# Attention scores of a unit accumulated in one PSUM bank per head with key differences, and some additions of exponentials moved to VectorE

## The chip, the cores and the metric

The kernel runs on one core of a Trainium2 chip. The metric is the device time of one execution in microseconds (us). The median of three runs of the kernel before is 2413.94 us (2413.16 to 2414.01). The profile shows one profiled execution of the same program; its span is 2411.0 us.

The names of the engines in the profile: PE is TensorE (matmuls), PEld its weight loads, DVE is VectorE, ACT is ScalarE, POOL is GpSimd, and SP is SyncE, which here only issues transfers (DMAs).

## What is computed

One transformer block with adaptive layer norm. B = 2 rows of T = 2048 tokens, D = 512, H = 16 heads of HD = 32, everything in float32:

```
mod = silu(condition) @ Wada + bada           # six vectors of D per row
xm  = layernorm(x) * (1 + sc_a) + sh_a
q, k, v = split(xm @ Wqkv)                    # 16 heads of 32
s   = (q . k) * 32**-0.5, causal
x   = x + gt_a * (softmax(s) @ v @ Wproj + bproj)
xm  = layernorm(x) * (1 + sc_m) + sh_m
x   = x + gt_m * (gelu(xm @ W1 + b1) @ W2 + b2)
```

## The kernel before

The program goes through these stages: Q, K and V products of row 0 (class `Qkv`), attention of row 0 (`attention_phase`), projection of row 0 together with the first norms of row 1 (`project_phase`), Q, K and V products of row 1, attention of row 1, its projection, and the MLP of both rows. Each engine works through its own queue in order. A scheduler places most instructions; matmuls (helper `mm`, so that all matmuls have the line L199) and those given to the helper `act` keep the order of the program text. All DMAs of attention and of the products are issued by SP, whose queue is in order too.

**Q, K and V products** (`Qkv.group`, L795 to L838; one group g is 512 tokens, four groups a row). A group makes for each chunk f of four heads one Q and one K product (each 128 x 512, f = 0 to 3), and then four V products. Scores are wanted in more than one rounded part, so every Q and K product is split into a high part, rounded to the matmul's short float format, and a low remainder: ACT writes `hl[:, 0]` from PSUM (L814), VectorE the remainder `hl[:, 1]` (L815), and SP stores the pair, 512 KB, to DRAM (L820). The tag `hl` has 4 buffers. V goes by ACT (L836) to the tile `vv`. The products use six PSUM banks, and the scores of the max pass (below) that already run between them use the two banks `s`.

In the same stages GpSimd prepares weights of the MLP (class `Quarters`): for each of sixteen "rooms", six in row 0 and ten in row 1, it loads pieces of W1 or W2 (L923), adds them in pairs (L931) and stores the sums to DRAM (L911).

**Attention.** The unit of work is (c, i): four heads c (HC = 4) by a block of QB = 512 queries i. There are 16 units a row. For every unit three things are done at different times:

- The max pass, three units ahead (AHEAD = 3). `Row.score` takes the next block of `todo`; `bank` (L435 to L455) makes a matmul of 128 queries against up to 512 keys into a bank `s`, and VectorE takes the maxima, with a plain reduction (L454) or, on the causal diagonal, with a masked one (L449). `due` spreads these blocks over the steps by a cost per step, and so decides how many, `n`, fall into each step. In steps with three or more blocks every other one borrows one of the four banks of `st` (`st_bank`).
- `rows` (L506) brings the negated maxima of a unit, in two rounded parts, into the tile `fold`, laid out so that a matmul with the selector `sel` writes the maximum of each query to all key rows of a bank.
- The scores themselves, transposed (keys on partitions), one step per key tile of 128 keys (`scores_t`, L538 to L597). In a step each of the four heads takes a bank `st`; the `sel` matmul (L563) starts it with the negated maxima, the keys' matmul (L571) adds K q, ACT takes the exponential into a tile `e` (L579), and on diagonal tiles GpSimd zeroes the masked part (L585).

The contraction of the scores uses 128 partitions: the high and low parts of Q and K, four times 32 rows. Two steps later (LAG = 2) the four tiles `e` are multiplied with V into the bank `o`. Their sums are first added up in tiles `ee`, up to four key tiles in a chain, by GpSimd (`add`, L605 to L607), or in the last unit of a row by VectorE; then a matmul with ones sums them over keys into the bank `sm`. `finish` divides.

A unit with query block i has 4i + 1 full key tiles and then the three tiles of the diagonal that are 384, 256 and 128 queries wide. They make two more steps: 384 and 128 together in one bank, then 256 (`steps_of`):

```
[(i * TQ + 1, P), (i * TQ + 3, 3 * P)], [(i * TQ + 2, 2 * P)]
```

The keys of a chunk (`kst`, 4 MB, two buffers) are loaded by SP, for chunk 0 as the groups are made, for the others at the head of the chunk before.

The Python loop over units and steps (L668) sets the order around the change: `scores_t` of the step with its blocks of the max pass, then `flush`, which issues the value matmuls of two steps before, then whatever is left of the blocks.

Of the kernel before, what the change touches and what calls it, by code (L numbers as in the profile page):

```python
# [27 lines left out]
def dit_block_kernel(  # L28
# [55 lines left out]
    def pool(name, bufs=1, **kw):  # L84
# [21 lines left out]
    tmask = bp.tile([P, TQ + 1], F32, tag="tmask", name="tmask")  # L106
    nc.vector.tensor_reduce(
        tmask[:, :TQ],
# [4 lines left out]
    nc.vector.tensor_copy(tmask[:, TQ:], tmask[:, TQ - 1 : TQ])  # L113
    fold, mhl = [], []
    for n in range(2):

        f = bp.tile([P, QB + P], F32R, tag=f"fold{n}", name=f"fold{n}")
        fold.append(f)
# [9 lines left out]
    def picks():  # L128
# [35 lines left out]
        [dram.tile([2, P, T], F32, tag=f"k{b}{c}", name=f"k{b}{c}") for c in range(C)]  # L164
        for b in range(B)
# [116 lines left out]
    class Row:  # L282


        def __init__(self, b):
            self.b = b
            self.vv = bp.tile([P, NT, D], F32, tag="vv", name="vv")
            self.kst, self.qst, self.pools = {}, {}, {0: bp}
# [12 lines left out]
        def load_keys(self, c, g, n=1):  # L301

            tok = slice(g * MT, (g + n) * MT)
            if g == 0:
                self.kst[c] = self.pools[c % 2].tile(
                    [P, HC, T], F32R, tag=f"kst{c % 2}", name="kst"
                )
            for r in range(4):
                nc.sync.dma_start(
                    self.kst[c][r * HD : (r + 1) * HD, :, tok].bitcast(F32),  # L310
                    kd[self.b][c][r % 2, :, tok].rearrange("(h d) t -> d h t", d=HD),
                )
# [122 lines left out]
        def bank(self, u, h, t, kb, s):  # L435
# [6 lines left out]
                self.kst[c][:, h, kb * QB : kb * QB + w],  # L442
# [41 lines left out]
        def score(self, n, borrow=None):  # L484

            for k in range(n):
                if borrow and k % 2 == 0:  # L490
                    s = borrow()
                else:
                    s = ps_sp.tile([P, QB], F32, tag="s", name="s")
                item = self.todo.pop(0)
                u = item[0]
                if self.mx is None:
                    self.mx = bp.tile(
                        [P, HC * TQ, units[u][1] + 1], F32, tag="mx", name="mx", bufs=3
                    )
                self.bank(*item, s)  # L500
                if not self.todo or self.todo[0][0] != u:
                    self.split(u, self.mx, s)
                    self.mx = None
                    self.at += 1

        def rows(self, u):  # L506
# [8 lines left out]
                fold[u % 2].rearrange("p (t q) -> p t q", t=TQ + 1),  # L515
                ps.unsqueeze(1).to_broadcast([P, TQ + 1, P]),
                tmask.unsqueeze(2).to_broadcast([P, TQ + 1, P]),
# [11 lines left out]
    def attention_phase(row):  # L529
        b, vv, kst, qst = row.b, row.vv, row.kst, row.qst  # L530
        with pool(f"att{b}") as ap, pool(
            f"ps_st{b}", bufs=HC, space=PSUM
        ) as ps_stp, pool(f"ps_o{b}", space=PSUM) as ps_op:
            row.pools[1] = ap

            n_bank = [0]

            def scores_t(u, step, n):  # L538
# [6 lines left out]

                def st_bank():

                    n_bank[0] += u == len(units) - 1  # L550
                    if n_bank[0] % 6 >= HC:
                        return ps_sp.tile([P, QB], F32, tag="s", name="st")
                    return ps_stp.tile([P, QB], F32, tag="st", name="st")

                c, i = units[u]
                tiles = steps_of[u][step]
                q0 = tiles[0][1]
                w = sum(QB - q for _, q in tiles)
                sts, es = [], []
                for h in range(HC):  # L560
                    g = slice(h * HD, (h + 1) * HD)
                    st = st_bank()
                    mm(  # L563
                        st[:, :w], sel[g, :], fold[u % 2][g, q0 : q0 + w],
                        start=True, stop=False,
                    )
                    sts.append(st)
                for h in range(HC):
                    at = 0
                    for j, q in tiles:  # L570
                        mm(  # L571
                            sts[h][:, at : at + QB - q],
                            kst[c][:, h, j * P : (j + 1) * P],
                            qst[u][:, h, q:],
                            start=False, stop=at + QB - q == w,
                        )
                        at += QB - q
                    e = ap.tile([P, QB], F32, tag="e", name="e", bufs=E_BUFS)
                    act(nc.scalar.activation(e[:, :w], sts[h][:, :w], AF.Exp))  # L579
                    if tiles[0][0] >= i * TQ:  # L580

                        d = e.rearrange("p (t k) -> p t k", k=P)[:, 0 : TQ : TQ - 1, :]
                        d = d[:, : len(tiles), :]
                        act(
                            nc.gpsimd.affine_select(  # L585
                                d, d, pattern=[[0, len(tiles)], [1, P]],
                                compare_op=ALU.is_ge, fill=0.0,
                                base=0, channel_multiplier=-1,
                            )
                        )  # L590
                    es.append(e)
                    if h < 2 and n >= 3 or h >= HC - n and n < 3:
                        row.score(1)
                if n >= 3:
                    row.score(1, st_bank)
                    row.score(min(n, HC) - 3)
                return es, max(0, n - HC)  # L597
# [6 lines left out]

            def add(u, h, dst, x, y):  # L605
                engine = nc.vector if u == len(units) - 1 else nc.gpsimd
# [924 lines left out]
```

## Time and profile before

| stage | stretch, us | PE busy | DVE busy | ACT busy | POOL busy |
|---|---|---|---|---|---|
| Q, K, V of row 0 | 0 to 216 | 205.17 | 111.96 | 44.39 | 48.34 |
| a piece of attention, row 0 | 360 to 500 | 139.67 | 97.20 | 76.93 | 119.52 |
| Q, K, V of row 1 | 812 to 1004 | 191.72 | 102.14 | 37.75 | 64.25 |
| attention, row 1 | 1004 to 1543 | 535.13 | 362.96 | 302.37 | 434.02 |
| MLP | 1603 to 2411 | 797.24 | 328.79 | 198.09 | 81.30 |
| whole span | 2411.0 | 2381.4 | 1345.9 | 896.4 | 1125.3 |

The profiled execution spans 2411.0 us; the page has no other time of its own for it. The median of the unprofiled runs lies 2.94 us above that span. In the answers quoted below, "idle" in brackets is the time for which an engine stood still before an instruction, and behind the arrow is what ended it; "(+1 forms)" tells that a row mixes shapes; the rows of busy time by stretch give, behind the stretch, the busy us of PE, PEld, DVE, ACT and POOL with instruction counts, the granted TensorE clock (1.00 is full), the DMA share and GB/s. Durations of one instruction are in ns in the groups and in us in timelines.

### The profile page before, as it was taken

The numbers are of one execution on the slowest core, as the hardware profiler recorded it, in microseconds if no ns is written. First come the engines' busy times: TensorE is split into PE (matmuls) and PEld (weight loads), VectorE is DVE, ScalarE is ACT, GpSimd is POOL, SyncE is SP. The second block draws the span as 40 slices with busy tenths as digits, with TensorE's granted clock in tenths as the row PEclk, the third lists the DMA queues.
The fourth block names the chain that finished last, engine by engine and source line by source line (L and its number), as shares of the span: only waits on it lengthen the run. The fifth ranks groups of instructions, "written<-read, shape, count | busy, mean of one in ns | idle before, by whom it ended". The sixth has DMA issues, their size and how long they took to land.

```text
span 2411.0 us, 31023 instructions
## 1 busy us (share of the span) xinstructions
PE 2381.4 (99%) x10797; PEld 1167.1 (48%) x10797; DVE 1345.9 (56%) x2813; ACT 896.4 (37%) x1671; POOL 1125.3 (47%) x1279
## 2 busy tenths in 40 slices
PE   8999999999999999999999999999999999999998
PEld 4455555555544445555555554444444444444443
DVE  3466666766647446766676665663344263343424
ACT  2113555555563121355555555423213212312310
POOL 1062888978775560199897878432001101100200
PEclk9999999999999999999999999999999999999999
DMA  7677124051325794621505132552324233222323
GB/s 253 197 239 198 41 47 96 23 118 42 111 96 186 240 319 162 154 55 34 111 23 115 45 101 91 168 178 77 110 78 146 76 106 136 82 92 87 122 87 101
DMA packets 132854, 285.72 MB, mean 119 GB/s; under 512 B 13472, under 2 KB 42700, under 8 KB 127832
## 3 DMA queue, kind: packets, MB, share of 16 engines
q1 hardware_dynamic: 125936, 256.94, 36.1%
q0 software_dynamic: 6384, 26.25, 3.1%
q8 instruction: 85, 1.39, 0.2%
q14 instruction: 73, 0.60, 0.1%
q10 hardware_dynamic: 376, 0.55, 0.1%
HBM read 209.76 MB, written 81.79 MB: 121 GB/s over the span
## 4 chain that ended last, share of the span: by engine, by line
PE 96%; DVE 2%; POOL 1%; issue 0%; DMA 0%; ACT 0%; SPq 0%; DVEq 0%; POOLq 0%; ACTq 0%
PE st L199 19%; PE ps_h L199 16%; PE ps_y L199 16%; PE o L199 11%; PE s L199 10%; PE ps_qk L199 9%; PE ps_o L199 5%; PE ps_v L199 4%; PE sm L199 4%; PE ps_xt L207 1%; POOL ee L607 1%; PE ps_o L207 1%; DMA x<-in_x_dram 0%; DVE junk L449 0%; DVE mx L454 0%
## 5 line engine op out<-in xcount | busy, mean ns | idle before, releaser
L579 ACT ACTIVATE e<-st 128x512 f32<-128x512 f32 (+1 forms) x1152 | 574.7, 578 | 427.1 <-PE st L199 359.7
L607 POOL TENSOR_TENSOR ee<-ee,e 128x512 f32<-128x512 f32 x424 | 529.8, 1294 | 4.3 <-ACT e L579 4.0
L454 DVE TENSOR_REDUCE mx<-s 128x1 f32<-128x512 f32 x604 | 407.6, 687 | 203.6 <-PE s L199 202.5
L199 PE MATMUL s<-kst,qst 128*128 128x512 f32 (+3 forms) x1032 | 463.8, 451 | 4.7 <-DVE mx L454 2.9
L199 PE MATMUL st<-qst,kst 128*128 128x512 f32 (+3 forms) x1280 | 409.2, 387 | 0.0
L1295 POOL TENSOR_TENSOR c<-c 128x512 f32<-128x512 f32 x32 | 40.7, 1272 | 623.2 <-DVE c L1257 596.6
L199 PE MATMUL o<-e,vv 128*32 128x512 f32 (+3 forms) x2560 | 300.6, 538 | 2.0 <-POOL e L585 2.0
L199 PE MATMUL ps_h<-sx,w 128*128 128x512 f32 x640 | 286.7, 592 | 0.0
L449 DVE CUSTOM_DVE_ANT_0 junk<-s,causal 128x512 bf16<-128x512 f32 (+3 forms) x428 | 209.0, 488 | 132.9 <-PE s L199 125.2
L199 PE MATMUL ps_y<-sh,w 128*128 128x512 f32 x640 | 277.6, 592 | 0.0
L199 PEld LDWEIGHTS st<-qst,kst 128*128 128x128 f32 x1280 | 227.4, 188 | 94.2 <-issue 62.1
L199 PEld LDWEIGHTS s<-kst,qst 128*128 128x128 f32 x1032 | 194.4, 189 | 154.4 <-DVE mx L454 55.2
L607 POOL TENSOR_TENSOR ee<-e 128x512 f32<-128x512 f32 x168 | 210.6, 1288 | 100.8 <-ACT e L579 100.3
L199 PE MATMUL ps_qk<-xmT,wqkv 128*128 128x512 f32 x512 | 239.0, 594 | 1.8 <-DVE xmT L256 1.8
L1257 DVE TENSOR_TENSOR h<-c,ps_h 128x512 f32<-128x512 f32 x128 | 88.1, 688 | 232.4 <-PE ps_h L199 232.4
L585 POOL TENSOR_SCALAR_AFFINE_SELECT e<-e 128x128 f32<-128x128 f32 (+1 forms) x384 | 123.0, 364 | 195.7 <-ACT e L579 193.0
L199 PEld LDWEIGHTS ps_h<-sx,w 128*128 128x128 f32 x640 | 121.1, 190 | 150.2 <-issue 149.7
L199 PEld LDWEIGHTS ps_y<-sh,w 128*128 128x128 f32 x640 | 120.3, 190 | 144.9 <-issue 143.5
L1281 ACT ACTIVATE h<-h,cols 128x512 f32<-128x512 f32 x128 | 92.4, 722 | 182.0 <-DVE h L1257 182.0
L199 PE MATMUL st<-fold,sel 32*128 32x512 f32 (+1 forms) x1152 | 148.6, 481 | 0.6 <-ACT vv L836 0.2
L199 PEld LDWEIGHTS ps_qk<-xmT,wqkv 128*128 128x128 f32 x512 | 93.9, 190 | 96.9 <-issue 90.4
L199 PEld LDWEIGHTS st<-fold,sel 32*128 32x128 f32 x1152 | 59.1, 181 | 144.2 <-ACT e L579 86.6
(129 smaller groups left out, 2359.9 us busy)
## 6 DMA issues: line engine op xcount, KB each, us to landing
qst<-q SPq DMA_DIRECT2D x128, 256.0 KB
w<-w1d SPq DMA_DIRECT2D x34, 896.0 KB
w<-w2d SPq DMA_DIRECT2D x28, 1024.0 KB
kst<-k SPq DMA_DIRECT2D x24, 1024.0 KB
q<-hl SPq DMA_DIRECT2D x32, 512.0 KB
k<-hl SPq DMA_DIRECT2D x32, 512.0 KB
kst<-k SPq DMA_DIRECT2D x32, 256.0 KB
w<-in_L_cond_W_dram POOLq DMA_DIRECT2D x64, 128.0 KB, 5.6
```

What stands on the lines that cost most here:

```text
L199: return tc.keep_in_program_order(nc.tensor.matmul(*args, **kw))
L207: return tc.keep_in_program_order(nc.tensor.transpose(dst, src, ident[:n, :n]))
L449: nc.vector.tensor_tensor_reduce(junk[:, :w], s[:, :w], causal[:, QB - w :], 1.0, MASKED, ALU.add, ALU.max, m,)
L454: nc.vector.tensor_reduce(m, s[:, :w], axis=AX.X, op=ALU.max)
L579: act(nc.scalar.activation(e[:, :w], sts[h][:, :w], AF.Exp))
L585: nc.gpsimd.affine_select(d, d, pattern=[[0, len(tiles)], [1, P]], compare_op=ALU.is_ge, fill=0.0, base=0, channel_multiplier=-1,)
L607: act(engine.tensor_tensor(dst, x, y, ALU.add))
L1257: nc.vector.tensor_tensor(dst, x, y, op)
L1281: nc.scalar.activation(d, d, AF.Gelu, bias=col(r_b1 + chunk, 1))
L1295: nc.gpsimd.tensor_tensor(c1_, c1_, c2_, ALU.subtract)
```

## The change

1. **Key differences.** The four banks `st` are taken once per unit, one per head. The `sel` matmul stands only at the first key tile of a unit (and at every tile of the first unit of a row). For a later tile j the program adds (K_j - K_(j-1)) q to the same bank, so that it holds K_j q minus the maximum again; the exponential reads the bank between two additions. Unit 0 keeps `kst`; the others read the differences from a new tile `kgap`.
2. **Order of the diagonal.** Since the tiles are taken in turn, the last two steps are now the 384-wide tile, and the 256- and the 128-wide one, in this order. The value matmuls of an earlier step are issued between those two. Each has an exponential of its own.
3. **Making the differences.** `Qkv.gaps` forms them from each K product: GpSimd sets or copies the last 128 columns of the group before, ACT copies the product from PSUM, GpSimd keeps the new last columns (`tails`), VectorE subtracts, ACT rounds the high part, GpSimd subtracts the low part, and SP stores 512 KB to `gd`. The pair tile `dl` shares the tag `hl`, whose buffers go from 4 to 3.
4. **Max pass.** No banks are borrowed any more; all blocks use the two banks `s`, one after `h` = 0, one after `h` = 1, one after the fourth head, and the others behind the value matmuls.
5. **Loads.** `kst` has one buffer and is loaded head by head behind the last block of a head in the max pass (`load_head`); `kgap` is loaded in four pieces per chunk (`load_gaps`), each of four transfers of 256 KB.
6. **Additions.** In every second chain the addition of the fourth head is made by VectorE, issued behind the next `scores_t`: 76 of GpSimd's 592.
7. `fold` is 512 instead of 640 wide.

```
-            def scores_t(u, step, n):
+            def scores_t(u, step, n, sts, values):
...
                 tiles = steps_of[u][step]
+                keys = row.kgap if u else kst
+                es = [
+                    ap.tile([P, QB], F32, tag="e", name="e", bufs=E_BUFS)
+                    for _ in range(HC)
+                ]
+                at = 0
+                for k, (j, q) in enumerate(tiles):
+                    if k:
+                        values()
+                    if j == 0 or u == 0:
+                        for h in range(HC):
+                            g = slice(h * HD, (h + 1) * HD)
+                            mm(
+                                sts[h][:, q:], sel[g, :], fold[u % 2][g, q:],
+                                start=True, stop=False,
+                            )
+                    for h in range(HC):
                         mm(
-                            sts[h][:, at : at + QB - q],
-                            kst[c][:, h, j * P : (j + 1) * P],
+                            sts[h][:, q:],
+                            keys[:, h, j * P : (j + 1) * P],
                             qst[u][:, h, q:],
-                            start=False, stop=at + QB - q == w,
+                            start=False, stop=True,
+                            skip_group_check=u > 0 and j > 0,
                         )
...
+                        if not k and (h < 2 and n >= 3 or h >= HC - n and n < 3):
+                            row.score(1)
+                    if not k and n >= 3:
                         row.score(1)
-                if n >= 3:
-                    row.score(1, st_bank)
-                    row.score(min(n, HC) - 3)
-                return es, max(0, n - HC)
+                    at += QB - q
+                return es, max(0, n - 3)
...
             def add(u, h, dst, x, y):
-                engine = nc.vector if u == len(units) - 1 else nc.gpsimd
-                act(engine.tensor_tensor(dst, x, y, ALU.add))
+                if u == len(units) - 1:
+                    act(nc.vector.tensor_tensor(dst, x, y, ALU.add))
+                elif h == HC - 1 and n_chain[0] % 2:
+                    late.append(
+                        lambda: act(nc.vector.tensor_tensor(dst, x, y, ALU.add))
+                    )
+                else:
+                    act(nc.gpsimd.tensor_tensor(dst, x, y, ALU.add))
...
-                + [[(i * TQ + 1, P), (i * TQ + 3, 3 * P)], [(i * TQ + 2, 2 * P)]]
+                + [[(i * TQ + 1, P)], [(i * TQ + 2, 2 * P), (i * TQ + 3, 3 * P)]]
...
+                    if u % NQ == NQ - 1 and c + 1 < C and n_step in (5, 9, 13):
+                        row.load_gaps(c + 1, n_step // TQ - 1)
+                    elif u % NQ == 0 and c and n_step == 1:
+                        row.load_gaps(c, NG - 1)
...
-                    es, rest = scores_t(u, n_step, n)
+                    es, rest = scores_t(u, n_step, n, sts, lambda: flush(now))
+                    add_late()
...
+        def gaps(self, g, f, ps, hp, tok):
+            kf = hp.tile([P, P + MT], F32, tag="kf", name="kf", bufs=2)
+            tail = self.tails[:, f, :]
+            if g == 0:
+                nc.gpsimd.memset(kf[:, :P], 0.0)
+            else:
+                nc.gpsimd.tensor_copy(kf[:, :P], tail)
+            nc.scalar.copy(kf[:, P:], ps)
+            if g + 1 < NG:
+                nc.gpsimd.tensor_copy(tail, kf[:, MT:])
+            d = kf[:, :MT]
+            nc.vector.tensor_tensor(d, kf[:, P:], d, ALU.subtract)
+            dl = hp.tile([P, 2, MT], F32R, tag="hl", name="dl", bufs=3)
+            nc.scalar.copy(dl[:, 0, :], d)
+            nc.gpsimd.tensor_tensor(dl[:, 1, :], d, dl[:, 0, :].bitcast(F32), ALU.subtract)
+            nc.sync.dma_start(
+                gd[self.row.b][f][:, :, tok].rearrange("l p t -> p l t"), dl.bitcast(F32)
+            )
...
-                    hl = hp.tile([P, 2, MT], F32R, tag="hl", name="hl", bufs=4)
+                    hl = hp.tile([P, 2, MT], F32R, tag="hl", name="hl", bufs=3)
...
+                    if which == 1:
+                        self.gaps(g, f, ps, hp, tok)
...
+        def load_head(self, c, h):
+            for r in range(4):
+                nc.sync.dma_start(
+                    self.kst[r * HD : (r + 1) * HD, h, :].bitcast(F32),
+                    kd[self.b][c][r % 2, h * HD : (h + 1) * HD, :],
+                )
+
+        def load_gaps(self, c, g):
+            tok = slice(g * MT, (g + 1) * MT)
+            for r in range(4):
+                nc.sync.dma_start(
+                    self.kgap[r * HD : (r + 1) * HD, :, tok].bitcast(F32),
+                    gd[self.b][c][r % 2, :, tok].rearrange("(h d) t -> d h t", d=HD),
+                )
...
-        def score(self, n, borrow=None):
+        def score(self, n):
...
+                if i == NQ - 1 and c + 1 < C and self.todo[0][:2] != (u, h):
+                    self.load_head(c + 1, h)
```

## The prediction

> **What bounds the kernel now.** I read the busy times and the chain of the end first, then busy time by stretch, then the rows of the operations that the change touches, then two timelines. The page's busy times and chain:
>
> ```profile
> PE 2381.4 (99%) x10797; PEld 1167.1 (48%) x10797; DVE 1345.9 (56%) x2813; ACT 896.4 (37%) x1671; POOL 1125.3 (47%) x1279
> ...
> PEclk9999999999999999999999999999999999999999
> ...
> PE 96%; DVE 2%; POOL 1%; issue 0%; DMA 0%; ACT 0%; SPq 0%; DVEq 0%; POOLq 0%; ACTq 0%
> ```
>
> TensorE is busy 99% of 2411.0 us, carries 96% of the chain, and its granted clock stays full. Whatever leaves TensorE shortens the kernel by at most its own time, and whatever makes TensorE wait lengthens it in full. The stretches (windows; time, then busy us of each engine) are the Q/K/V products of row 0 (0 to 216), a middle piece of its attention, and the Q/K/V products of row 1 (812 to 1004):
>
> ```profile
> 0.00:216.00 216.00, 205.17 (x622) 101.87 (x622) 111.96 (x279) 44.39 (x79) 48.34 (x82) 1.00 0.70 224
> ...
> 360.00:500.00 140.00, 139.67 (x957) 73.00 (x956) 97.20 (x242) 76.93 (x154) 119.52 (x135) 1.00 0.33 73
> ...
> 812.00:1004.00 192.00, 191.72 (x541) 95.23 (x540) 102.14 (x237) 37.75 (x69) 64.25 (x101) 1.00 0.70 222
> ```
>
> In attention GpSimd is at 85% and VectorE at 69%. In the product stretches both have room on average; the order of their queues is what counts there. Rows of the touched operations (page, costliest groups):
>
> ```profile
> L607 POOL TENSOR_TENSOR ee<-ee,e 128x512 f32<-128x512 f32 x424 | 529.8, 1294 | 4.3 <-ACT e L579 4.0
> ...
> L199 PE MATMUL s<-kst,qst 128*128 128x512 f32 (+3 forms) x1032 | 463.8, 451 | 4.7 <-DVE mx L454 2.9
> ...
> L199 PE MATMUL st<-fold,sel 32*128 32x512 f32 (+1 forms) x1152 | 148.6, 481 | 0.6 <-ACT vv L836 0.2
> ```
>
> **The step of attention.** Timeline of one step, from one group of `sel` to the next:
>
> ```profile
> 603.43 0.50 PE L199 MATMUL st<-fold,sel 32*128 32x512 f32 x4
> ...
> 603.87 0.50 PE L199 MATMUL st<-qst,kst 128*128 128x512 f32 x1
> ...
> 604.20 0.40 PE L199 MATMUL s<-kst,qst 128*128 128x512 f32 x1
> ...
> 604.63 0.69 DVE L454 TENSOR_REDUCE mx<-s 128x1 f32<-128x512 f32 x1 [0.40 <-PE s L199]
> ...
> 605.32 0.40 PE L199 MATMUL st<-kst,qst 128*128 128x512 f32 x1
> ...
> 605.88 1.07 PE L199 MATMUL o<-e,vv 128*32 128x512 f32 x8
> ...
> 606.88 0.50 PE L199 MATMUL st<-fold,sel 32*128 32x512 f32 x4
> ```
>
> The four `sel` matmuls take 0.44 us (603.43 to 603.87) of 3.45. A score starts its reduction 0.43 us later (604.20 to 604.63), the reduction takes 0.69, and successors follow about every 0.61. The matmul `st<-kst,qst` at 605.32 is a max-pass score in a borrowed bank.
>
> **Part 1: `sel` groups.** The changed program issues 38 groups of four instead of 288. 250 x 0.44 = 110 us leave TensorE, the row's own busy time saying 148.6 x 250/288 = 129. This is gross. Four things take some back.
> (a) Two banks for the max pass: after K0 s K1 s K2 K3 s come the values, and one or two more scores right behind them. With 0.43 + 0.69 us from a score to its free bank, walking the order with these intervals, the step of four scores (88 of them) falls from 3.41 to about 3.15 rather than 2.98: 0.17 x 88 = 15 back. The step of five (68) needs 5 x 0.61 = 3.05 of reductions that now bunch at the seam of two steps; it falls from about 3.75 to 3.65, so 0.34 x 68 = 23 back. Ends: nothing back, or all 110 (VectorE sets the step).
> (b) A unit's `sel` now waits for the exponential of the last, 128-wide tile of the same bank: about 0.6 us at 28 unit ends, 17 back (0 to 28 x 1.2).
> (c) The last two steps have three exponentials per head instead of two; 30 units x 0.25 us for the extra seam, 7.5 back (0 to 15).
> (d) The last unit of each row has no max pass; its step took 2.55, its four exponentials 2.07 and its four VectorE additions about 2.5, so removing 0.44 from 28 steps yields only half: 6 back (0 to 12).
> Sum: 110 - 15 - 23 - 17 - 7.5 - 6 = about 41 us gained.
>
> **Part 2: additions on VectorE.** 76 additions leave GpSimd (76 x 1.29 = 98 us of its time, off the path) for VectorE, where the same shape has a median of 0.68 us and a maximum of 1.78. A step leaves VectorE some 0.8 us after its third reduction, so I take zero. Behind the addition on VectorE stand the next reductions, and TensorE's score waits for those. Bounds: zero, and 76 x 1.09 = 83 us, if each lasts as the longest did. What speaks for delays is that 1.78. [...]
>
> **Part 3: key differences in the product stretches.** Per K product (16 a row) the change adds ACT 2 x 0.60, VectorE 0.69, GpSimd a subtraction of 1.29 plus two 128-wide copies, and a 512 KB store from SP; the ring of `hl` shrinks to three buffers that rotate so that every difference `dl` takes the same one. On average all fits (ACT 44 of 216 us). The order doesn't. In the changed program's GpSimd queue the low-part subtraction of group 2, f=2, stands behind the second and third room of MLP weights, and those rooms are paced by their own DMAs. Timeline of GpSimd, row 0:
>
> ```profile
> 149.22 4.27 POOL L923 DMA_DIRECT2D w<-in_L_cond_W_dram  x6 [3.88 <-DMA w1d<-w]
> ...
> 168.22 4.28 POOL L923 DMA_DIRECT2D w<-in_L_cond_W_dram  x6 [3.90 <-DMA w1d<-w]
> ...
> 185.23 0.58 POOL L911 DMA_DIRECT2D w1d<-w  x1 [0.30 <-POOL w L931]
> ```
>
> Room 3 starts at 168.2 and issues its last store at 185.2. The subtraction then ends near 187.3; its store needs about 5 us (the longest wait of a key load for a `hl` store is 4.9), so the buffer is free near 192. ACT's copy of the next difference (f=3) waits for it, and ACT, in order, holds behind it the high part of group 3's first Q; VectorE, in order, holds the low part of that Q ahead of the max-pass reductions; two `s` banks fill and TensorE stops where it was at 172 and resumes near 197: 25 us. An earlier hold of about 9 us (group 2, f=0 behind room 1) lies inside these 25. In row 1 the subtraction of group 0, f=2, stands behind seven rooms:
>
> ```profile
> 880.84 0.55 POOL L911 DMA_DIRECT2D w2d<-w  x1
> ...
> 890.15 0.58 POOL L911 DMA_DIRECT2D w2d<-w  x1 [0.30 <-POOL w L931]
> ```
>
> 880.8 + 1.3 + 5 puts ACT's next copy at 887 and the score that stood at 865.9 at about 889; the following difference stands behind the eighth room (890.2), which puts the score of 873.1 at about 900: 27 us. A ring of three for a store of 5 us costs another 4 us in the groups without rooms. Loss: 25 + 27 + 4 = 56 us. Below: 46, if the 4 don't appear and the stores land 3 us sooner in each of two waits; nothing at all, if the order doesn't bite as I read it (rival B). Above: 80, because the stores' 8.4 MB a row are 37 us at the 224 GB/s of this stretch, and two thirds of that, 24 us, could stretch the rooms.
>
> **Part 4: loads and edits with one answer.** `kgap` adds 64 loads of 256 KB a row, 16.8 MB in 539 us or 31 GB/s on top of 73 at a DMA share of 0.33: hidden. Sixteen of them stand at the head of attention on SP; unit 1 needs the first four, unit 0 covers them: 0, at most 2 x 6 us. `kst` is loaded head by head behind the head's last score and first read after the other three heads' scores (some 8 us against 5 for a landing): 0, at most 6 loads x 3 us. The narrower `fold` saves a fifth of 0.82 us x 32 on VectorE, 5 us off the path: 0.
>
> **Sum.** 2411.0 - 41 + 56 = 2426. The median of three runs, 2413.94, lies 2.94 above the span; with it 2429 us, +0.6%. A measurement of this kernel tells 0.2%, 4.8 us, from no change.
>
> **Rivals.**
> A. The two banks don't stall TensorE. For it: in the whole run scores wait only 2.9 us for VectorE's maxima, and many blocks are narrower than 512. Against: those 2.9 are with borrowed banks and 0.44 us of `sel` as slack in every step. Time: 2414 - 110 + 56 = 2360, faster. It decides from 61 us of gain on. [...]
> B. The waits of part 3 don't occur, because ACT's copy for f=3 comes free earlier than the rooms let me think. For it: TensorE waited just 1.8 us in the products; against: the rooms' times. Time: 2414 - 41 = 2373, faster. With A too, 2304.
> C. VectorE's additions are held by GpSimd's and hold the reductions: 0.5 us for each of 76 gives 38 on top, 2467; with the full bounds of part 3, about 2484. It decides at 0.2 us each.
>
> **Chances.** Forecast (both mechanisms as worked out, own range 2405 to 2465) 0.50, of which 0.38 slower, 0.07 within, 0.05 faster; A 0.17; B 0.12; A and B 0.03; C 0.18. Faster 0.05 + 0.17 + 0.12 + 0.03 = 0.37; within 0.07; slower 0.38 + 0.18 = 0.56. That the change removes no `sel` is excluded by the count of instructions. The range 2352 to 2484 reaches over A, B and C and leaves out A with B and the tails.
>
> **What would show it.** Right: `sel` x152; the idle time ahead of `s` for VectorE's maxima grows from 2.9 us to tens; in each product stretch a gap of some 25 us on TensorE behind a full `s`, with ACT waiting for the DMA of `dl` and GpSimd for its weight loads; the first stretch ends near 245 and the second lasts near 220; attention takes about 518 instead of 539 us a row. Wrong: an attention of 485 us (A), product stretches of 216 and 192 (B), or additions on VectorE well over 0.7 us on the mean in the middle of attention (C).

## The result, and the profile after

The changed kernel takes 2531.25 us (median; 2529.95 to 2532.02), the kernel before 2413.98 beside it: ratio 1.0486, 95% interval 1.0471 to 1.05. It is slower by 117 us; the forecast had a slower kernel as the likelier outcome, but by 15 us, and the top of its range was 2484. The span of the profiled execution is 2530.3 us, 119.3 more than before.

From the profile page of the changed kernel (busy times, granted clock, the chain of the end by engine, the score row of the costliest groups):

```profile
PE 2360.9 (93%) x9797; PEld 1113.4 (44%) x9797; DVE 1462.1 (58%) x2920; ACT 971.2 (38%) x1863; POOL 1121.1 (44%) x1291
...
PEclk9998999999999989999999999999999999999999
...
PE 77%; DVE 12%; DMA 5%; POOL 4%; issue 2%; ACT 0%; SPq 0%; DVEq 0%; ACTq 0%; POOLq 0%
...
L202 PE MATMUL s<-kst,qst 128*128 128x512 f32 (+3 forms) x1280 | 591.8, 474 | 129.3 <-DVE mx L472 66.8
```

TensorE carried 96% of the chain; now it carries 77%, and VectorE, transfers and GpSimd took over 21%. Ahead of the scores of the max pass (`s`) TensorE stands idle for 129.3 us, where it was 4.7.

Where the time lies is read from the first `sel` matmul and the first projection matmul of each row, taken from the timelines of TensorE (us):

| stage | before | changed | difference |
|---|---|---|---|
| to the first score step, row 0 (products) | 212.8 | 248.2 | +35.4 |
| attention, row 0 | 542.4 | 568.0 | +25.7 |
| projection of row 0, products of row 1 | 246.9 | 278.3 | +31.5 |
| attention, row 1 | 541.4 | 568.3 | +26.9 |
| the rest (projection, MLP) | 867.6 | 867.4 | -0.1 |

The two product stretches lose 67 us, and attention, which was to gain 41, loses 53. The MLP is untouched.

**The product stretches.** Timeline of the changed kernel around the stop in row 0 (start, duration, engine, instruction; in brackets how long the engine had stood idle, and for what):

```profile
195.89 0.59 POOL L966 DMA_DIRECT2D w1d<-w  x1 [0.30 <-POOL w L986]
...
196.73 1.27 POOL L843 TENSOR_TENSOR dl<-kf,dl 128x512 fp32r<-128x512 f32 x1
...
201.34 0.62 ACT L842 CAST dl<-kf 128x512 fp32r<-128x512 f32 x1 [20.69 <-DMA g<-dl]
...
205.99 0.80 PE L202 MATMUL s<-kst,qst 128*128 128x512 f32 x1 [20.31 <-DVE mx L472]
```

This is the forecast's path, link by link: GpSimd makes the low part only behind the last store of the third weight room, ACT's next copy waits 20.69 us for that buffer's store, and TensorE stands for 20.31 us in front of a score. In row 1 the same stop lasts 20.69 us, at 949. A smaller hold of 7.2 us, the transposes waiting for `xn`, comes at 145. It isn't the one that the prediction named behind the first room: ACT's split of a product just ahead of it waits 5.5 us for the store of a K pair (`k<-hl`), and in run 2 below, with GpSimd out of the path, that wait (5.4 us) and the hold (7.8 us) are still there. It belongs to the buffers and their stores.

The stop has a second price, which was not in the forecast. Windows of the changed kernel (busy us of PE, PEld, DVE, ACT and POOL, then the granted TensorE clock, the DMA share and GB/s):

```profile
180.00:186.00 6.00, 5.69 (x15) 2.37 (x13) 0.71 (x2) 0.59 (x1) 3.79 (x6) 1.00 0.40 140
186.00:192.00 6.00, 0.00 (x0) 0.00 (x0) 0.00 (x0) 0.00 (x0) 5.94 (x10) 0.86 0.26 82
192.00:198.00 6.00, 0.00 (x0) 0.00 (x0) 0.00 (x0) 0.00 (x0) 5.57 (x8) 0.50 0.62 249
...
207.00:210.00 3.00, 3.00 (x6) 1.34 (x4) 2.00 (x5) 1.05 (x2) 1.56 (x2) 0.50 0.79 255
210.00:213.00 3.00, 3.00 (x9) 1.51 (x8) 1.24 (x4) 0.00 (x0) 0.00 (x0) 0.87 0.98 303
213.00:216.00 3.00, 3.00 (x10) 1.52 (x9) 2.32 (x5) 1.10 (x2) 0.00 (x0) 1.00 0.95 196
```

While TensorE stands, its granted clock falls to 0.50, and it is back at 1.00 only some 5 us after the first matmul; the pairs of product matmuls take 1.91 us instead of 1.02 until then. Half speed for 5 us adds, as an estimate, about 2.5 us to each long stop. Read in windows of 1 us, the clock is halved 4.6 us after the last matmul in row 0 and 2.6 us after it in row 1, and full again 4.8 and 5.8 us after the start of the next one.

**Attention.** Windows over the attention of row 0, before and after:

```profile
212.80:755.10 542.30, 538.13 (x3666) 277.77 (x3665) 364.27 (x863) 304.44 (x608) 434.84 (x493) 1.00 0.31 79
```

```profile
248.17:816.21 568.04, 521.74 (x3167) 248.92 (x3166) 410.83 (x903) 324.21 (x673) 406.32 (x456) 0.99 0.43 108
```

500 matmul records fewer, VectorE 47 us more. Waits of the weight loads (PEld) of TensorE in the same stretches show better than its idle time what holds it, because part of the waiting is counted as busy (in run 3 the matmuls of row 0's attention, the same 3666 as before, count 566 us busy instead of 538); before:

```profile
PEld s L199 <- DVE mx L454: 25.8, 36, 0.8
PEld s L199 <- DVE mx L449: 15.3, 22, 0.8
```

and after:

```profile
PEld s L202 <- DVE mx L472: 112.6, 190, 2.0
PEld s L202 <- DVE mx L467: 49.9, 86, 1.9
PEld o L202 <- issue: 38.6, 136, 0.8
PEld st L202 <- ACT e L587: 24.4, 39, 0.8
```

The loads of the scores wait 162 us a row for VectorE's maxima, four times as long as before. Waiting for an exponential is no new cost (45.0 us before, 24.4 after), nor are the added loads: ahead of the products with `kgap` TensorE stands idle for 0.9 us in the whole run. The additions on VectorE, from the groups of tile `ee` (min, median and max ns):

```profile
L626 POOL TENSOR_TENSOR ee<-ee,e x370: 1260/1290/1750, 272.9 to 1616.6; 128x512 f32<-128x512 f32 x185
...
L620 DVE TENSOR_TENSOR ee<-ee,e x56: 670/680/1756, 778.4 to 1655.2; 128x512 f32<-128x512 f32 x56
L623 DVE TENSOR_TENSOR ee<-ee,e x54: 679/926/1790, 278.5 to 1613.8; 128x512 f32<-128x512 f32 x54
L620 DVE TENSOR_TENSOR ee<-e x24: 674/682/1772, 774.3 to 1646.2; 128x512 f32<-128x512 f32 x24
L623 DVE TENSOR_TENSOR ee<-e x22: 1141/1513/1762, 274.4 to 1605.2; 128x512 f32<-128x512 f32 x22
```

Alone on VectorE, in the last unit (L620), an addition takes 0.68 us at the median. The moved ones (L623), beside GpSimd's, take 0.93 and 1.51. Rival C is there; how much of the loss it makes, the first experiment says.

### The profile page after: what moved, and what is told of

Read it like the earlier page. It is cut to its first block, busy times and chain, and to the rows that moved or that the text cites. A ratio compares the mean times of both kernels' runs of the same rounds, so it can differ in the third digit from the quotient of the medians.

```text
span 2530.3 us, 29489 instructions
## 1 busy us (share of the span) xinstructions
PE 2360.9 (93%) x9797; PEld 1113.4 (44%) x9797; DVE 1462.1 (58%) x2920; ACT 971.2 (38%) x1863; POOL 1121.1 (44%) x1291
## 4 chain that ended last, share of the span: by engine, by line
PE 77%; DVE 12%; DMA 5%; POOL 4%; issue 2%; ACT 0%; SPq 0%; DVEq 0%; ACTq 0%; POOLq 0%
PE ps_h L202 15%; PE ps_y L202 15%; PE s L202 11%; PE o L202 8%; PE st L202 8%; PE ps_qk L202 6%; DVE mx L472 5%; PE ps_o L202 4%; PE sm L202 4%; PE ps_v L202 3%; DVE junk L467 3%; DVE ee L623 2%; POOL w L986 2%; DMA w<-in_L_cond_W_dram 1%; PE ps_xt L210 1%
## 5 line engine op out<-in xcount | busy, mean ns | idle before, releaser
L587 ACT ACTIVATE e<-st 128x512 f32<-128x512 f32 (+3 forms) x1280 | 610.4, 535 | 439.2 <-PE st L202 382.4
L202 PE MATMUL s<-kst,qst 128*128 128x512 f32 (+3 forms) x1280 | 591.8, 474 | 129.3 <-DVE mx L472 66.8
L472 DVE TENSOR_REDUCE mx<-s 128x1 f32<-128x512 f32 x768 | 518.1, 688 | 186.6 <-PE s L202 178.1
L626 POOL TENSOR_TENSOR ee<-ee,e 128x512 f32<-128x512 f32 x370 | 484.1, 1349 | 22.3 <-ACT e L587 22.2
L202 PEld LDWEIGHTS s<-kst,qst 128*128 128x128 f32 x1280 | 236.8, 190 | 484.1 <-DVE mx L472 253.0
L202 PE MATMUL st<-qst,kgap 128*128 128x512 f32 (+3 forms) x1248 | 393.4, 376 | 0.9 <-DMA kgap<-g 0.9
L467 DVE CUSTOM_DVE_ANT_0 junk<-s,causal 128x128 bf16<-128x128 f32 (+3 forms) x512 | 248.6, 485 | 128.6 <-PE s L202 119.0
L202 PEld LDWEIGHTS st<-qst,kgap 128*128 128x128 f32 x1248 | 222.1, 189 | 78.6 <-ACT e L587 43.4
L626 POOL TENSOR_TENSOR ee<-e 128x512 f32<-128x512 f32 x146 | 183.0, 1286 | 131.1 <-ACT e L587 131.1
L202 PE MATMUL ps_v<-wqkv,xmT 128*128 128x512 f32 x256 | 122.8, 596 | 2.8 <-ACT xmT L264 2.8
```

What stands on the lines that cost most here:

```text
L202: return tc.keep_in_program_order(nc.tensor.matmul(*args, **kw))
L467: nc.vector.tensor_tensor_reduce(junk[:, :w], s[:, :w], causal[:, QB - w :], 1.0, MASKED, ALU.add, ALU.max, m,)
L472: nc.vector.tensor_reduce(m, s[:, :w], axis=AX.X, op=ALU.max)
L587: nc.scalar.activation(es[h][:, at : at + QB - q], sts[h][:, q:], AF.Exp)
L626: act(nc.gpsimd.tensor_tensor(dst, x, y, ALU.add))
```

## The experiments

Theory 1: in attention the max pass, with two banks instead of two and the borrowed ones, couples TensorE to VectorE's pace, and that eats the removed matmuls; the additions on VectorE are a smaller part; in the product stretches GpSimd's order is the cause. Rivals: the additions are all of it; ACT's chain or the added loads; the ring of three buffers. The stage times stand in the order of the table above, without the last line, which stays at 867 us everywhere.

**1. The additions back on GpSimd.**

```
-                elif h == HC - 1 and n_chain[0] % 2:
-                    late.append(
-                        lambda: act(nc.vector.tensor_tensor(dst, x, y, ALU.add))
-                    )
```

> The changed kernel with all 76 late additions back on GpSimd. Theory 1 (two banks and VectorE's pace hold TensorE in attention, the additions are a smaller part): the 76 additions took about 83 us of VectorE, some half of it on the path; attention 568 to about 550 us a row, total 2531 to 2490-2505. Theory 2 (the additions, held by GpSimd's, are the whole of the loss in attention): attention 530 us a row or less, total 2455 or less. Theory 3 (the loss in attention comes from ACT's chain or from the loads of differences): attention stays at 565-570, total within 5 us of 2531.

2514.45 us (1.042, 1.0403 to 1.0438); stages 249.3, 555.5, 278.4, 558.6. The additions cost 12.5 and 9.7 us in attention, 22 in all: 0.29 us each. They are a part, not the whole; theory 2 falls. Attention is still 13 to 17 us longer than before, with 55 us a row less of `sel`.

**2. Differences made without GpSimd.**

```
-            nc.gpsimd.tensor_tensor(dl[:, 1, :], d, ...)
+            nc.vector.tensor_tensor(dl[:, 1, :], d, ...)
...
-                nc.gpsimd.tensor_copy(tail, kf[:, MT:])
+                nc.scalar.copy(tail, kf[:, MT:])
```

(and the other copy of the tails by ACT, the zeros by VectorE)

> The changed kernel with nothing of the making of the differences on GpSimd: low part by VectorE, tails by ACT. If GpSimd's order behind the weight rooms makes the loss of 67 us in the product stretches: first score step at 215-225 instead of 248 us, second stretch (projection, products) 247-258 instead of 278 us, total about 2475. If the ring of three buffers, SP's queue or the added transfers make it: first score step still past 235 us, total above 2515.

2495.64 us (1.0334, 1.0319 to 1.035); stages 230.1, 566.5, 259.2, 569.8. Both 20 us stops are gone, the stretches shrink by 18.1 and 19.1 us. So GpSimd's part in the differences makes 37 of the 67 us. What is left, 17.3 and 12.3, is more than expected.

**3. Two banks in the kernel before.** The borrowing is taken out; the blocks stand as in the changed kernel.

```
-                    if n_bank[0] % 6 >= HC:
+                    if False:
...
-                    row.score(1, st_bank)
-                    row.score(min(n, HC) - 3)
-                return es, max(0, n - HC)
+                    row.score(1)
+                return es, max(0, n - 3)
```

> The kernel before, but its max pass uses only the two banks s, in the order of the changed kernel (third block behind the fourth head, the others behind the value matmuls). If two banks hold TensorE to VectorE's pace, attention rises from 542 to 560-590 us a row even with sel in every step, and TensorE's idle time ahead of s rises from about 1.5 us a row to over 15; total 2450-2510. If the banks don't matter (rival): attention within 5 us of 542, total within 10 us of 2414.

2488.51 us (1.0303, 1.0288 to 1.0319); stages 214.9, 579.0, 247.5, 578.2. Two banks alone cost 36.6 and 36.8 us a row, with every `sel` matmul, every addition and every transfer as before. The waits of the score loads for VectorE, row 0:

```profile
PEld s L199 <- DVE mx L454: 68.4, 138, 1.1
...
PEld s L199 <- DVE mx L449: 23.2, 46, 0.8
```

91.6 us instead of 41.1. This is the core of the answer: the step of four blocks goes from 3.43 us to 3.80 (medians of the steps without sums, from TensorE's timeline); without `sel`, as in run 1, it is 3.41. The removal pays 0.39 us a step, and the lost banks take 0.37.

**4 and 5. Less work for VectorE.** The plain reductions read 128 of 512 columns (maxima over the others are left out):

```
-                nc.vector.tensor_reduce(m, s[:, :w], axis=AX.X, op=ALU.max)
+                nc.vector.tensor_reduce(m, s[:, :P], axis=AX.X, op=ALU.max)
```

> The changed kernel with the plain reductions of the max pass reading 128 of their 512 columns: it leaves out the maxima over the other columns, TensorE's work is unchanged. A plain reduction falls from 0.69 to about 0.29 us, which frees some 0.4 us x 768 = 300 us of VectorE. If VectorE's pace behind two banks holds TensorE: attention 568 to 490-515 us a row, total 2531 to about 2410. If ACT, GpSimd or the loads hold it: attention above 555 us, total above 2505.

2456.03 us (1.0174, 1.015 to 1.0199); stages 250.0, 533.1, 276.8, 536.1: 32 to 35 us a row come back, not the 53 and more that were expected. Then the masked reductions as well, and the additions back on GpSimd:

```
-                    junk[:, :w], s[:, :w], causal[:, QB - w :],
+                    junk[:, :P], s[:, :P], causal[:, QB - P :],
```

> The changed kernel with late additions back on GpSimd and with both kinds of reduction of the max pass, plain and masked, reading 128 columns: it leaves out the maxima over the other columns. If VectorE between two banks is all that keeps the removed matmuls from paying (542 less 55 a row): attention 490-505 us a row, total 2371-2400. If about 15 us a row or more lie elsewhere (the seam of the units, the last three tiles, the wait of a bank for its exponential): attention 505-530 us, total 2400-2450.

2447.8 us (1.0138, 1.0123 to 1.0154); stages 251.4, 523.8, 276.9, 532.1. The step of four blocks takes 3.06 us, that of five 3.16; the removal of 0.44 us alone would leave 2.98 and 3.31. With VectorE's work in the attention of row 0 halved (from 411 to 207 us) attention gains 9 to 19 us a row on before, against 55 of `sel`. The rest lies elsewhere, as the second branch had it.

**6. The same with the additions on VectorE.**

> As the run with both reductions narrowed to 128 columns (maxima over the other columns left out), but with the late additions on VectorE as in the changed kernel. If GpSimd's queue is what kept that run at 524-532 us of attention a row: 505-520 us here, and less waiting of the value matmuls for the masked e than 9 us a row. If the seams of the units or something else kept it: 520 us or more.

2451.05 us (1.0142, 1.0113 to 1.0172); stages 249.5, 526.5, 277.0, 532.3. No difference to run 5 within its spread: the value matmuls' own waits for masked `e` fall from 9.4 us a row to 2.1, but in row 0 one addition on VectorE now takes 7.05 us (352.75 to 359.80); it ends 0.55 us after the last of five that GpSimd makes without a break. GpSimd's queue isn't what keeps attention above 520.

**7. A third bank.** On top of run 10 below (additions on GpSimd, differences without it), the sums of the exponentials go into the bank of the values, so that both outputs are mixed up; TensorE and VectorE do the same work. The products have five banks instead of six, and their stretches take 5.2 and 5.6 us more than in run 10.

```
-    ps_s_cm = pool("ps_s", bufs=2, space=PSUM)
+    ps_s_cm = pool("ps_s", bufs=3, space=PSUM)
...
-                        sm = ps_op.tile([P, QB], F32, tag="sm", name="sm")
+                        sm = o
```

> Additions on GpSimd and differences made without it, as in the run with two repairs, and the sums of the exponentials are accumulated into the bank of the values (both outputs are thereby mixed up), so that the max pass has a third bank; the products have five banks instead of six. TensorE's and VectorE's work is unchanged. If the number of banks is what lets VectorE hold TensorE: attention 556 to 525-540 us a row, close to the 524-532 with VectorE's work cut. If VectorE's amount of work holds it with any number of banks: attention stays above 548 us.

2419.62 us (1.0021, 1.0012 to 1.0031); stages 234.4, 522.2, 267.4, 524.7. Windows of the attention of row 0, first run 10, with two banks, then this one:

```profile
229.23:785.32 556.09, 520.22 (x3166) 248.69 (x3166) 369.09 (x866) 324.06 (x673) 437.28 (x493) 1.00 0.44 110
```

```profile
234.41:756.61 522.20, 502.04 (x3165) 260.58 (x3165) 353.58 (x862) 309.82 (x671) 436.94 (x493) 1.00 0.47 116
```

The waits of the score loads for VectorE, row 0, in the same two runs:

```profile
PEld s L202 <- DVE mx L472: 108.1, 194, 1.1
PEld s L202 <- DVE mx L467: 44.6, 86, 1.1
```

```profile
PEld s L202 <- DVE mx L472: 52.2, 82, 0.8
PEld s L202 <- DVE mx L467: 30.9, 49, 0.8
```

One bank is worth 33.9 and 35.0 us a row, with the same reductions to be made. It brings the step of four to about 3.05 us, the same as cutting VectorE's work does (run 5). So VectorE's amount of work as such isn't the limit: with that work unchanged, a third block on its way is enough. With two, as these runs are read here, the time from a score to the end of its reduction (0.43 + 0.69 us in the prediction's timeline) sets the pace. The waits that remain, 83 us, are longer than those before, so a wait of a load is not in itself time lost.

**8. Blocks spread over the step.** In steps with three or more, one block behind the first and third head's keys, one behind the first and third head's value matmuls.

```
                         es[h][:, at : at + QB - q0], start=first, stop=last,
                     )
+                    if h % 2 == 0 and len(row.todo) > floor[0]:
+                        row.score(1)
```

> The changed kernel with its max-pass blocks spread over the step: in steps with three or more, one behind the first and one behind the third head's keys, one behind the first and one behind the third head's value matmuls, the rest at the end. Work and banks are the same. If the loss in attention comes from blocks that follow each other closer than the two banks come free: attention falls from 568 to 530-550 us a row, total to 2460-2495. If VectorE's whole amount of work or the late additions set it, wherever the blocks stand: attention within 6 us of 568, total within 12 us of 2531.

2870.88 us (1.1887, 1.187 to 1.1905); attention 733.9 and 739.5. Neither branch; the timeline of TensorE shows why:

```profile
474.15 1.05 PE L202 MATMUL o<-e,vv 128*32 128x512 f32 x4
475.13 0.49 PE L202 MATMUL s<-kst,qst 128*128 128x512 f32 x1
475.56 1.05 PE L202 MATMUL o<-e,vv 128*32 128x512 f32 x2
476.54 0.50 PE L202 MATMUL s<-kst,qst 128*128 128x512 f32 x1
```

The eight value matmuls of four heads, each with 32 columns of weights, take 1.06 us when they stand together (the prediction's timeline has them: `x8`, 1.07). Two of them, or four, between other matmuls take 1.05 too. So eight together cost no more than two alone, and a group of eight that two blocks cut into three takes some 3 us, estimated from these 1.05. The run says nothing on bunching.

The same order with the additions on GpSimd and the differences made without it:

> Three repairs together on the changed kernel: no late additions, differences made without GpSimd, max-pass blocks spread over the step. If the three causes add up (12 us a row, 18 us a stretch, and 20 or more us a row for the spread): 2531 - 23 - 36 - 40 = about 2430, near the time of before; if the spread does more in the absence of late additions, 2390-2415, a kernel faster than before. If the spread does nothing: about 2475.

2837.11 us (1.1751), attention 735.6 and 739.5, for the same reason.

**9. The value matmuls kept together, but put between the second and the third head's keys.**

```
+                        if len(tiles) == 1 and n >= 3 and h == 1:
+                            values()
+                            row.score(1)
+                        if len(tiles) == 1 and n >= 4 and h == 2:
+                            row.score(1)
```

> The changed kernel with the four value matmuls, kept together, moved between the second and the third head's keys in steps with three or more max-pass blocks of a single tile; a block follows directly behind them and one behind the third head. No two pairs of blocks then stand closer than the value matmuls' 1.0 us. If it is the bunching of blocks at the seam of two steps that two banks can't take: the step of four blocks falls from 3.5 to 3.1-3.25 us, attention from 568 to 535-555 us a row, total 2465-2510. If the sum of VectorE's work per step sets the pace: step of four at 3.4 or more, total within 10 us of 2531.

2549.85 us (1.0563, 1.0545 to 1.0582); attention 576.0 and 570.9. The step of four falls from about 3.5 to 3.3 us, that of five rises from about 3.8 to 4.0 (medians). Shifting blocks within the step moves the stall; it doesn't remove it.

**10. Two repairs** (runs 1 and 2 together):

> Late additions on GpSimd and differences made without GpSimd, order of the step as changed. If these two causes are independent, as theory 1 has it: 2531 - 17 - 36 = about 2478, attention 553-559 us a row, first score step near 230 us. If they overlap: 2490 or more.

2476.04 us (1.0255, 1.024 to 1.0271); stages 229.2, 556.1, 261.8, 559.7. The two causes add up: 2531 - 17 - 36 = 2478, within 3 us.

**11. Three repairs**, run 10 with the order of run 9 and the scratch of `split` in SBUF:

> Three repairs on the changed kernel: late additions on GpSimd, differences made without GpSimd, value matmuls between the second and third head's keys (and the scratch of the split of maxima in SBUF instead of a bank s). If they add up: 2531 - 23 - 36 - 20 to 60 = 2412 to 2452, about the time of before or a little slower. If GpSimd, busy 439 of 555 us with all additions, becomes the next to hold TensorE: above 2450.

2505.39 us (1.0384); attention 570.7 and 577.4, slower than run 10. The scratch alone, on run 10:

```
-            m = s[:, : HC * TQ].rearrange("p (h t) -> p h t", h=HC)
+            m = bp.tile([P, HC * TQ], F32, tag="mxs", name="mxs", bufs=2)
```

> Two repairs (additions on GpSimd, differences made without it) and the scratch of the split of a unit's maxima in SBUF instead of in the last bank s, which frees that bank some 0.6 us earlier once a unit. At most 16 x 0.6 us a row: total 2476 to 2460-2470; if the split doesn't hold a bank that is wanted: 2473-2479.

2499.19 us (1.0347, 1.0332 to 1.0362); attention 567.9 and 570.9: 11 to 12 us a row slower, where a gain or nothing was expected. The timelines of VectorE and GpSimd at one of these places:

```profile
646.34 7.03 DVE L489 TENSOR_TENSOR mhl<-mxs,mhl 128x16 fp32r<-128x16 f32 x1
...
647.19 6.15 POOL L623 TENSOR_TENSOR ee<-ee,e 128x512 f32<-128x512 f32 x5
```

The subtraction of 16 columns, 0.17 us at its shortest, takes 7.03 us: it ends with the last of five additions that GpSimd makes without a break (647.19 + 6.15 = 653.34; 646.34 + 7.03 = 653.37). With the scratch in PSUM (run 10) it had one operand in SBUF, and all 32 took 0.16 to 0.18; with both in SBUF, the 32 take 0.17 to 7.05, 0.35 at the median. In the attention of row 0 four take over 1 us: 1.03, 1.10, 5.92 and 7.03. The moved additions, with both operands in SBUF as well, show waits for one addition: in the changed kernel's timeline 56 of the 76 start while GpSimd has an addition in hand, and these take 0.81 to 1.79 us; 54 of them end 0.55 us after it. The other 20 take 0.68 to 0.77.

**12. The ring.** The kernel before with two buffers of `hl` instead of four, so that a buffer is used again after two products, as often as in the changed kernel.

```
-                    hl = hp.tile([P, 2, MT], F32R, tag="hl", name="hl", bufs=4)
+                    hl = hp.tile([P, 2, MT], F32R, tag="hl", name="hl", bufs=2)
```

> The kernel before with two buffers of hl instead of four, so that a buffer is used again after two products, as it is in the changed kernel with three buffers for three pairs per chunk. If the shorter ring makes the part of the loss in the product stretches that GpSimd's order doesn't (17 and 12 us): first score step at 222-232 instead of 213 us, total 2430-2445. If the ring doesn't matter: total within 5 us of 2414.

2427.25 us (1.0048, 1.0032 to 1.0065); stages 218.1, 542.2, 255.6, 542.2. The ring costs 5.3 and 8.7 us, between the two cases expected: 14 of the 30 that run 2 leaves, if it costs as much there. The other 16, most of it in row 0, were not taken apart; the hold of 7.8 us for `xn` in run 2, behind ACT's wait for a store of a K pair, is not in this run.

None of these kernels is faster than the one before.

## Why the prediction was right or wrong

**Product stretches: right in mechanism, size within its bounds.** Forecast 56 us, at most 80; measured 67. The split was off: 52 were given to GpSimd's order and 4 to the ring; run 2 measures 37 for the order and run 12 measures 14 for the ring, and 16 stay open. In row 1 the two waits that made the forecast's 27 us were one stop of 20.69. The end of the first stretch, named as near 245, was 248; the second, named as near 220, lasts 221 from its first product (873.6) to the first score step (1094.5). Rival B falls.

**Part 1(a): the step that failed.** Taken back by two banks: 38 us were forecast, 69 were measured (third bank, 33.9 + 35.0). The walk through the order used a full reduction of 0.69 and its successors every 0.61, and found a step of four at 3.15; it is 3.41 without the late additions, and 0.26 us in each of 88 steps is 23 of the missing 31. The step of five was about right (3.65; measured 3.5 to 3.7 at the median, by which steps are counted). Two things were missing from the walk. One is the steps that also hold sums or a `fold`. I had priced them at the whole 0.44 us of gain; they gain nothing or lose. A step of four that also holds one group of sums took 4.29 us before, 4.26 in run 10 and 3.85 with the third bank; a step of five that also holds the transpose of the maxima 3.89, 4.77 and 3.37 (medians). That transpose occupies one of the two banks too, and after the change the score loads wait 11 us a row for `fold`. The other, argued and not measured by itself, is that two banks form a loop: each stall of TensorE makes the next reduction start later, so that a hold anywhere is not made up for. Away from the ends of units (counted below) the rows take 317 and 316 us before, and 317 and 322 in run 10: there the two banks eat all that the removal gains. The bounds had been set right ("all 110: VectorE sets the step"), but the value taken lay too near the lower one.

**Parts 1(b) to (d).** 30.5 us were forecast. With the third bank, attention gains 20.2 + 16.7 = 37 us of the 110, so what isn't VectorE's pace takes 73. TensorE's timelines show that most of it lies at the ends of the units. The last two steps of a unit and the first two of the next hold nearly the same matmuls before and after, but for three groups of `sel` that are gone (1.3 us). Together they take 16.1 us before (mean of 14 a row) and 17.1 in run 10; with the third bank 17.0 to 17.1, and with VectorE's reductions cut (run 5) 16.7 to 17.0, so neither is what holds them. Where 1.3 us was to be gained, 0.9 to 1.0 is lost: some 32 and 31 us a row, of 35 and 38 that are missing in the third-bank run. In the other steps that run gains 33 and 29 us a row, of the 37 that their 83 groups are worth. So (b) and (c), 24.5 us, were too small as well: by this count the ends of the units take back some 63. What in them costs the time is open. In the third-bank run the value matmuls' waits for GpSimd's masks are a part (15.5 us in row 0, 3.3 in run 10, 1.0 before). Part (d) took nothing back: the step of a row's last unit, without blocks, fell from 2.55 to 2.12 us, the whole gain of a group.

**Part 2.** Zero was forecast, 22 us measured, 0.29 us for each addition. Rival C had put its point of decision at 0.2, so it took place, at about half of its price of 38. No run shows the 0.5 us an addition behind that price; run 1 shows 0.29 in its place. The maximum of 1.78 us in the row of additions was a better guide than its median of 0.68: the moved ones took 0.93 and 1.51 at the median.

**The sum.** 110 - 69 - 73 - 22 = -54 in attention, against +41; measured stage by stage -53. The 73 is a remainder, so this sum doesn't test the split. With the 67 of the products that makes the 119 us. Rival A was on the wrong side by as much: its evidence, 2.9 us of waiting for maxima before, was taken with the borrowed banks and with `sel` as slack, as the prediction's own counter-argument said, and run 3 shows that without the borrowed banks attention is 37 us a row longer. Rival C's upper time is 2491 by the prediction's own terms (2467 and 24 more for part 3), not 2484; the measured 2531 lies above both. Part 4's zero held: TensorE waited 0.9 us for the new loads.

## What to carry to other kernels

Count the buffers that a change takes away as carefully as the instructions. Here 110 us of matmuls were removed, and the bank that each head kept for a whole unit had been the slack of another pass: one bank was worth 34 us a row. To price a loop of producer and consumer over two buffers, take every user of these buffers into the walk, small ones too (a transpose, a scratch), and lean to the bad bound when the consumer is as busy as VectorE was here (69% in the middle of attention). Look at the ends of units by themselves, too: a mean step doesn't show them. And when new work is given to an engine with idle time, look at what stands ahead of it in its queue, not at its share of busy time.

## What the runs showed of the hardware

- Matmuls with 32 columns of weights for four heads, each into its own 32 rows of a bank: eight that follow each other take 1.06 us, and two or four alone, between full-width matmuls, take 1.05 as well (run 8).
- Operations of VectorE with both operands in SBUF took longer beside GpSimd's additions, at times as long as several of these: 0.17 us of work took 7.03 and ended with the last of five in a row (run 11). With one operand in PSUM none of the 32 took over 0.18 (run 10). Of the changed kernel's 76 moved additions, the 56 that started during one of GpSimd's took 0.81 to 1.79 us, the others 0.68 to 0.77.
- After stops of 20.31 and 20.69 us in the changed kernel TensorE's granted clock was at 0.50, and it was full again 4.8 and 5.8 us after the start of the next matmul.
- With a reduction of 0.69 us for each block, a third bank beside two shortened a step of four blocks from 3.41 us to 3.05 (runs 10 and 7).
